# A graph layer's segment sums on TensorE: one full-width product per edge tile, or seven on four column quarters

## The chip, the cores and the metric

The kernel runs on one core of a Trainium2 chip, in fp32 throughout. The metric is device time in microseconds (us) of one execution; three runs of the kernel before took 5686.64, 5694.77 and 5710.15 us.

## The reference

12500 nodes carry 160 channels: 64 scalars and 32 vectors of three components. 400000 edges, sorted by their destination, each carry a source node, 16 numbers (`e16`) and 4 numbers (`e4`).

```python
h = relu(layernorm(x))                                   # [12500, 160]
x0, x1 = h[:, :64], h[:, 64:].reshape(n, 32, 3)
s0, y0 = x0 @ W_sc0 * a / 8, x0 @ W_l1_0 * a / 8         # a: one number per node
s1, y1 = the same of x1 with W_sc1, W_l1_1, / sqrt(32)
w = silu(e16 @ fc_W1 / 4) @ fc_W2 / 8                    # [400000, 192]
w_a, w_b, w_c, w_d = w[:, :64], w[:, 64:128], w[:, 128:160], w[:, 160:]
e0, e1 = e4[:, :1], e4[:, 1:]
mid_a = w_a * y0[src] * e0                               # 64
mid_d = w_d * (y1[src] . e1) / sqrt(3)                   # 32
mid_b = (w_b * y0[src])[:, :, None] * e1[:, None, :]     # 64 x 3
mid_c = (w_c * e0)[:, :, None] * y1[src]                 # 32 x 3
z0 = segment sum over dst of [mid_a, mid_d]              # 96 per node
z1 = segment sum over dst of [mid_b, mid_c]              # 96 x 3 per node
out0 = C_S * s0 + C_X * z0 @ W_l2_0 * a * const          # 96 -> 64
out1 = C_S * s1 + C_X * z1 @ W_l2_1 * a * const          # 96 -> 32, for each of three components
result = x + [out0, out1]
```

The indices `src` and `dst` are known only at run time.

## The kernel before

**Node stage.** The 98 tiles of 128 nodes are normalised, turned and mapped; `y0, y1` go to the scratch `y_d` in DRAM, the rest into the table `acc` in SBUF. Weights are loaded here, on SP's queue, by `edge_weight_loads` (L201), and scaled by DVE in `edge_weights` (L219). Among them is `wo`, three slabs of 128 rows by 160 columns, which holds W_l2_0 and three copies of W_l2_1 laid out for the 384 sums of a node.

**Edge stage.** The 3125 tiles of 128 edges are taken four at a time: 782 blocks. Three consecutive tiles (a window) touch at most 32 consecutive nodes in the ordinary case; four windows, 12 tiles, three blocks, are a group, and there are 261 groups. For a block b the functions are these:

- `load` (L403): SP fetches `e16`, and POOL issues four gathers (L417), one per tile, of 128 rows of 160 numbers from `y_d`, into `yg`. There are ten yg buffers, and the loads run eight blocks ahead; each POOL gather of a new buffer waits until DVE is done with the block that had it.
- `hidden_pair` (L434): PE's first edge product (L426) and ACT's silu (L431), for four blocks at a time.
- `weigh` (L440): PE makes the 192 edge weights of each tile (L448, two row halves of the array), and ACT scales 96 of them by e0 (L368) and writes e1 and the edge's place in its window beside them (L369). The result stays in PSUM; two such buffers.
- `select` (L472): DVE writes, for each tile, a matrix of 128 edges by 4 x 32 columns: the fourth part has a one where the edge goes to that node of the window, the first three parts are it times a component of e1 (L479, L481).
- `products` (L484): six DVE instructions (L374 to L381) make the 256 numbers `pr` of each edge: columns 0 to 63 mid_a, 64 to 95 mid_d, 96 to 191 mid_c by component, 192 to 255 w_b * y0.
- `sums` (L491): one PE product per tile, stationary the 128 columns of `sel`, moving the 256 of `pr`; three tiles add up in a PSUM bank (two such banks). Rows 96 to 127 of the result hold the sums with the plain ones, of which columns 0 to 191 are wanted; rows 0 to 95 hold those times e1's components, of which columns 192 to 255 are wanted. ACT takes these four pieces out in four instructions per window (L504, three of L506) and lays them as 32 rows of 384 in `zs`.
- After a group, in the three blocks that follow: `turn` (L509) transposes `zs` in three pieces (L514) and ACT copies the result (L516); `linear` (L519) makes three PE products with `wo` (L523), ACT copies the result (L525), and DVE makes `place` (L527); `add` (L530) distributes the rows over two node tiles by PE (L535), and `accumulate` (L538) reads a register that tells which node tiles, and adds them into `acc` with two DVE instructions (L544).

**Order.** PE, ACT and DVE run in the order in which the program is written (a manual schedule); the tile framework sets the semaphores. In the loop over blocks (L568) the order is: load(b + 8), weigh(b + 2), one of turn, linear, add for the group before, select and products of b + 1, accumulate in a group's third block, sums(b), and hidden_pair in every fourth block. An fp32 matmul stands in the profile as two passes, each a weight load (PEld) and a product (PE). A last part of the program (from L600) deals with tiles whose nodes lie too far apart; it keeps `wo` and isn't entered with these inputs.

Of the kernel before, what the change touches and what calls it, by code (L numbers as in the profile page):

```python
# [10 lines left out]
F32 = mybir.dt.float32  # L11
I32 = mybir.dt.int32
AF = mybir.ActivationFunctionType
ALU = mybir.AluOpType
# [4 lines left out]
P = 128  # L19
M0 = 64  # L20
M1 = 32
# [4 lines left out]
PC = 256  # L26
ZC = 384
GT = 4
BT = 32
WN = 32  # L30
WT = 3
GW = 4
TG = WT * GW
EG = 8
GN = 8
HN = 2
LO = D - P
EPS = 1e-5
C_S = math.sin(math.pi / 8.0)
# [4 lines left out]
def kernel(  # L44
# [19 lines left out]
    nc = tc.nc  # L64
# [3 lines left out]
    T = n_edges // P  # L68
# [13 lines left out]
    const = ctx.enter_context(tc.tile_pool(name="const", bufs=1))  # L82
# [5 lines left out]
    ident = const.tile([P, P], F32, name="ident")  # L88
# [90 lines left out]
    w1 = const.tile([P, 2 * FC_H], F32, name="w1")  # L179
    w2 = const.tile([P, NW], F32, name="w2")  # L180

    wo = const.tile([P, 3, D], F32, name="wo")
    wnr = ip.tile([P, 2, 3 * M1], F32, name="wnr")
    wor = ip.tile([P, 3, D], F32, name="wor")
# [16 lines left out]
    def edge_weight_loads():  # L201
        nc.gpsimd.memset(w1, 0.0)
        for i in range(P // FC_IN):
            nc.sync.dma_start(w1[FC_IN * i:FC_IN * (i + 1), FC_H * (i % 2):FC_H * (i % 2 + 1)], fc_w1)
        for i in range(2):
            for to, of, m in ((0, 0, M0), (M0, 2 * M0, M1), (M0 + M1, M0, M0), (2 * M0 + M1, 2 * M0 + M1, M1)):
                nc.sync.dma_start(w2[FC_H * i:FC_H * (i + 1), to:to + m], fc_w2[:, of:of + m])
        nc.gpsimd.memset(wor, 0.0)

        def o1(c):  # L210
            return slice(M0 + M1 * c, M0 + M1 * (c + 1))

        nc.sync.dma_start(wor[0:M0 + M1, 0, 0:M0], w_l2_0)
        for rows, k, c in ((slice(96, P), 0, 0), (slice(0, 32), 1, 1), (slice(32, 64), 1, 2)):
            nc.sync.dma_start(wor[rows, k, o1(c)], w_l2_1[M0:, :])
        for rows, k, c in ((slice(64, P), 1, 0), (slice(0, 64), 2, 1), (slice(64, P), 2, 2)):
            nc.sync.dma_start(wor[rows, k, o1(c)], w_l2_1[0:M0, :])

    def edge_weights():  # L219
        nc.vector.tensor_scalar(w2, w2, 1.0 / math.sqrt(FC_H), None, ALU.mult)  # L220
        f = C_X / math.sqrt(10.0 * (M0 + M1))
        nc.vector.tensor_scalar(wo[:, :, 0:M0], wor[:, :, 0:M0], f, None, ALU.mult)
        nc.vector.tensor_scalar(wo[M0:M0 + M1, 0, 0:M0], wo[M0:M0 + M1, 0, 0:M0], 1.0 / math.sqrt(3.0), None, ALU.mult)
        nc.vector.tensor_scalar(wo[:, :, M0:].rearrange("p k (u c) -> p k c u", c=3),
                                wor[:, :, M0:].rearrange("p k (c u) -> p k c u", c=3), f, None, ALU.mult)
# [27 lines left out]
    with (  # L253
# [82 lines left out]
        with tc.manual_schedule(engines=engines):  # L336
# [7 lines left out]
            last = len(steps) - 1  # L344
# [38 lines left out]
    with (  # L383
# [16 lines left out]
        def windows_of(g):  # L400
            return min(GW, NWIN - g * GW)
# [87 lines left out]
            prs[b] = pr  # L489

        def sums(b):  # L491
            pr = prs.pop(b)
            for k, t in enumerate(tiles_of(b)):
                g, w = t // TG, t // WT % GW
                if t % WT == 0:
                    z_ps[g, w] = p_z.tile([P, 512], F32, name="pz")
                pz = z_ps[g, w]
                last = t % WT == WT - 1 or t == T - 1
                nc.tensor.matmul(pz[:, 0:PC], sels[g][:, t % TG, :, :], pr[:, k, :], start=t % WT == 0, stop=last)  # L499
                if last:  # L500
                    if w == 0:
                        z_sb[g] = post.tile([P, ZC], F32, name="zs")
                    pz, zs = z_ps.pop((g, w)), z_sb[g][WN * w:WN * (w + 1), :]
                    nc.scalar.activation(zs[:, 0:192], pz[96:P, 0:192], AF.Copy)  # L504
                    for c in range(3):
                        nc.scalar.activation(zs[:, 192 + M0 * c:192 + M0 * (c + 1)],  # L506
                                             pz[WN * c:WN * (c + 1), 192:PC], AF.Copy)

        def turn(g):  # L509

            m, zs = WN * windows_of(g), z_sb.pop(g)
            pt = p_x.tile([P, 3, P], F32, name="px")
            for k in range(3):
                nc.tensor.transpose(pt[:, k, :m], zs[:m, P * k:P * (k + 1)], ident[:m, :m])  # L514
            za = post.tile([P, 3, P], F32, name="za")
            nc.scalar.activation(za[:, :, :m], pt[:, :, :m], AF.Copy)  # L516
            zT[g] = za

        def linear(g):  # L519
            m, za = WN * windows_of(g), zT.pop(g)  # L520
            po = p_x.tile([P, D], F32, name="px")
            for k in range(3):
                nc.tensor.matmul(po[:m, :], za[:, k, :m], wo[:, k, :], start=k == 0, stop=k == 2)  # L523
            os = post.tile([P, D], F32, name="os")
            nc.scalar.activation(os[:m, :], po[:m, :], AF.Copy)  # L525
            place = post.tile([P, 2, P], F32, name="place")
            nc.vector.tensor_scalar(place.rearrange("p h n -> p (h n)"), iota, at[:, g:g + 1], None, ALU.is_equal)  # L527
            o_sb[g] = os, place
# [205 lines left out]
```

## Time and profile before

| what | us |
|---|---|
| three runs, median | 5694.77 |
| the profiled execution, its own time | 5716.56 |
| its span in the profile | 5714.8 |
| PE busy, products / weight loads | 3840.1 / 2679.8 |
| DVE busy | 2902.1 |
| ACT busy | 2645.1 |
| POOL busy | 3024.8 |
| PE idle before the turn (L514), most of it until ACT's L504 | 876.2 |
| DVE idle before L479, most of it until ACT's L369 | 951.5 |
| mean TensorE clock granted, share of full | 0.776 |

Busy times are those of one engine in one execution. PE's products are pipelined, so their durations overlap and their sum isn't time at the peak; what a pass costs is seen better in the distance of starts, or in how long a row of them lasts. "Idle before" is time in which the engine had nothing under way ahead of that instruction, and the name behind the arrow is what the profile takes to have ended the wait; "remote" means that it finds no releaser close to the moment the wait ended. A queue's own rows carry a q (SPq). The clock is a mean over stretches: in some the array runs at full speed, in others at half.

### The profile page before, as it was taken

The page shows a single profiled execution, that of the slowest core. Times are in us where ns is not written, and L with a number is a line of the kernel's source. Part 1 is how long each engine was busy: PE and PEld are TensorE (multiplying, and loading weights), DVE is VectorE, ACT ScalarE, POOL GpSimd, SP SyncE. Part 2 cuts the span into 40 slices and gives each one's busy share as a digit, 9 for nine tenths or more (in the row PEclk, how much of TensorE's full clock was granted, in tenths as well). Part 3 has the DMA queues.
Part 4 walks back from the last instruction along what each step waited for, and adds up shares of the span by engine and source line. Part 5 has one row for each costly group of instructions (what it writes and reads, how often), then busy time and mean ns, then how long its engine had stood idle before and what let it go on. Part 6 is the DMA issues. An engine that isn't in the chain of part 4 may idle for free.

```text
span 5714.8 us, 61466 instructions
## 1 busy us (share of the span) xinstructions
PE 3840.1 (67%) x17265; PEld 2679.8 (47%) x17265; DVE 2902.1 (51%) x7407; ACT 2645.1 (46%) x9217; POOL 3024.8 (53%) x3150
## 2 busy tenths in 40 slices
PE   6476676666666666666667667666667766666766
PEld 5344444444444444444444445444444444444544
DVE  7454455444455455454555445544445554545555
ACT  5244444444444444444444444444444444444445
POOL 3655555555555555555555555555555555555553
PEclk9677777787777777777777777777777778788778
DMA  4211111211111111111112112111111121232211
GB/s 140 62 53 52 53 54 49 54 52 52 52 51 54 52 53 52 52 53 50 54 53 55 51 53 55 52 52 52 51 52 52 54 54 53 54 88 55 55 49 54
DMA packets 233168, 319.85 MB, mean 56 GB/s; under 512 B 65754, under 2 KB 182566, under 8 KB 232566
## 3 DMA queue, kind: packets, MB, share of 16 engines
q0 software_dynamic: 150000, 256.20, 16.7%
q1 hardware_dynamic: 69026, 51.24, 3.1%
q10 hardware_dynamic: 13796, 8.44, 0.5%
q8 instruction: 139, 2.28, 0.2%
q14 instruction: 207, 1.70, 0.1%
HBM read 299.62 MB, written 16.00 MB: 55 GB/s over the span
## 4 chain that ended last, share of the span: by engine, by line
PE 52%; another core or an unknown queue 23%; ACT 13%; issue 8%; DVE 3%; DMA 0%; SPq 0%; DVEq 0%; ACTq 0%
PE pz L499 25%; PE pw L448 10%; PE px L426 6%; ACT pw L368 5%; PE px L514 4%; PE px L523 4%; ACT zs L506 3%; PE px L535 3%; ACT zs L504 2%; ACT pw L369 1%; ACT hT L431 0%; DVE h L283 0%; DVE tmp L376 0%; DVE tmp L374 0%
## 5 line engine op out<-in xcount | busy, mean ns | idle before, releaser
L417 POOL DMA_INDIRECT yg<-y_d,src_sb x3125 | 2983.4, 955 | 2542.2 <-DVE pr L381 1641.0
L499 PE MATMUL pz<-pr,sel 128*128 128x256 f32 x6250 | 1930.1, 462 | 151.1 <-ACT zs L506 114.2
L368 ACT ACTIVATE pw<-pw,ev 128x96 f32<-128x96 f32 x3125 | 985.3, 315 | 1679.1 <-remote 1048.8
L499 PEld LDWEIGHTS pz<-pr,sel 128*128 128x128 f32 x6250 | 1443.4, 242 | 406.4 <-ACT zs L506 132.4
L544 DVE SCALAR_TENSOR_TENSOR acc<-px,a_sb,acc 128x160 f32 x522 | 200.2, 384 | 1765.5 <-remote 1292.0
L514 PE MATMUL px<-ident,zs 128*128 128x128 f32 (+1 forms) x783 | 268.9, 428 | 876.2 <-ACT zs L504 804.3
L448 PE MATMUL pw<-w,hT 64*128 64x192 f32 x6250 | 839.2, 394 | 12.9 <-DVE pr L381 8.1
L448 PEld LDWEIGHTS pw<-w,hT 64*128 64x128 f32 x6250 | 579.6, 216 | 469.4 <-issue 269.8
L426 PE MATMUL px<-xe,w 32*128 32x512 f32 x782 | 415.6, 789 | 526.1 <-remote 422.1
L479 DVE TENSOR_TENSOR sel<-iota,pw 128x128 f32<-128x128 f32 x782 | 223.5, 286 | 951.5 <-ACT pw L369 591.7
L504 ACT ACTIVATE zs<-pz 32x192 f32<-32x192 f32 x1042 | 337.8, 324 | 776.2 <-PE pz L499 312.9
L506 ACT ACTIVATE zs<-pz 32x64 f32<-32x64 f32 x3126 | 669.8, 214 | 41.8
L514 PEld LDWEIGHTS px<-ident,zs 128*128 128x128 f32 (+1 forms) x783 | 130.3, 181 | 1025.9 <-ACT zs L504 857.1
L376 DVE TENSOR_REDUCE tmp<-tmp 128x128 f32<-128x384 f32 x782 | 463.5, 593 | 26.8
L481 DVE TENSOR_TENSOR sel<-sel,pw 128x384 f32<-128x384 f32 x782 | 432.5, 553 | 26.7
L379 DVE TENSOR_TENSOR pr<-pw,yg 128x384 f32<-128x384 f32 x782 | 427.9, 547 | 0.0
L374 DVE TENSOR_TENSOR tmp<-yg,pw 128x384 f32<-128x384 f32 x782 | 427.8, 547 | 0.0
L426 PEld LDWEIGHTS px<-xe,w 32*128 32x128 f32 x782 | 107.8, 227 | 678.2 <-remote 470.9
L535 PE MATMUL px<-os,place 128*128 128x160 f32 x1044 | 236.7, 354 | 207.0 <-issue 175.0
L431 ACT ACTIVATE hT<-px 128x512 f32<-128x512 f32 x391 | 221.6, 596 | 300.5 <-remote 194.0
L377 DVE TENSOR_TENSOR pr<-pw,yg 128x256 f32<-128x256 f32 x782 | 323.6, 414 | 0.0
L378 DVE TENSOR_TENSOR pr<-pw,yg 128x256 f32<-128x256 f32 x782 | 323.4, 414 | 0.0
(83 smaller groups left out, 1902.3 us busy)
## 6 DMA issues: line engine op xcount, KB each, us to landing
yg<-y_d,src_sb POOLq DMA_INDIRECT x3125
xe<-in_e SPq DMA_DIRECT2D x784, 32.0 KB
xt<-in_x SPq DMA_DIRECT2D x12, 640.0 KB
y_d<-ys ACTq DMA_DIRECT2D x12, 640.0 KB
out<-acc SPq DMA_DIRECT2D x11, 640.0 KB
raw<-in_e SPq DMA_DIRECT2D x32, 192.0 KB
dst_i<-in_dst SPq DMA_DIRECT2D x1, 1568.0 KB
src_sb<-in_src SPq DMA_DIRECT2D x1, 1568.0 KB
```

The source lines that it names most:

```text
L368: nc.scalar.activation(pw[:, k, 0:96], pw[:, k, 0:96], AF.Copy, scale=ev[:, k, 0:1])
L374: nc.vector.tensor_tensor(tmp[:, :n, 0:3, :], y1, wt[:, :n, NW:NW + 3].unsqueeze(3).to_broadcast([P, n, 3, M1]), ALU.mult)
L376: nc.vector.tensor_reduce(tmp[:, :n, 3, :], tmp[:, :n, 0:3, :].rearrange("p t c u -> p t u c"), AX.X, ALU.add)
L379: nc.vector.tensor_mul(pr[:, :n, 96:192].rearrange("p t (c u) -> p t c u", c=3), wt[:, :n, M0:96].unsqueeze(2).to_broadcast([P, n, 3, M1]) ...
L417: nc.gpsimd.indirect_dma_start(out=yg[:, k, :], out_offset=None, in_=y_d, in_offset=bass.IndirectOffsetOnAxis(ap=src_sb[:, t:t + 1], axis=0))
L426: nc.tensor.matmul(ph, w1[r, :], xe[r, :], start=True, stop=True)
L448: nc.tensor.matmul(pw[:, k, 0:NW], hT[r, o:o + P], w2[r, :], start=True, stop=True)
L481: nc.vector.tensor_tensor(sel[:, :, 0:3, :], sel[:, :, 3:4, :].to_broadcast([P, n, 3, WN]), wt[:, :n, NW:NW + 3].unsqueeze(3).to_broadcast ...
L499: nc.tensor.matmul(pz[:, 0:PC], sels[g][:, t % TG, :, :], pr[:, k, :], start=t % WT == 0, stop=last)
L504: nc.scalar.activation(zs[:, 0:192], pz[96:P, 0:192], AF.Copy)
L506: nc.scalar.activation(zs[:, 192 + M0 * c:192 + M0 * (c + 1)], pz[WN * c:WN * (c + 1), 192:PC], AF.Copy)
L514: nc.tensor.transpose(pt[:, k, :m], zs[:m, P * k:P * (k + 1)], ident[:m, :m])
```

## The change

`sums` no longer makes one product of 128 by 256 per tile. The 128 columns of PE are taken as four quarters of 32. Each quarter collects 96 channels for the 32 nodes of a window: quarters 0 to 2 one vector component each (64 columns of w_b * y0 with `sel` times that component, and 32 columns of mid_c of that component with the plain `sel`), quarter 3 the 96 scalar ones. That is seven products per tile. The four windows of a group lie side by side in one bank, 4 x 96 columns, and ACT takes all out in one instruction after the group's last tile. `turn` transposes 96 columns of each window, four pieces; in the result a quarter's channels lie on 96 partitions for all 128 nodes of the group. `linear` multiplies each quarter with its own map, 96 by 64 or 96 by 32, from a new weight tile `wz` (two more DMAs on SP and two more DVE scalings), and ACT writes the result in two instructions, the second of which puts the components in their order. `wo` stays for the last part.

```diff
+    wz = const.tile([M0 + M1, M0 + M1], F32, name="wz")
...
+        nc.sync.dma_start(wz[:, 0:M0], w_l2_0)
+        nc.sync.dma_start(wz[:, M0:], w_l2_1)
...
+        nc.vector.tensor_scalar(wz, wz, f, None, ALU.mult)
+        nc.vector.tensor_scalar(wz[M0:, 0:M0], wz[M0:, 0:M0], 1.0 / math.sqrt(3.0), None, ALU.mult)
...
         def sums(b):
             pr = prs.pop(b)
             for k, t in enumerate(tiles_of(b)):
                 g, w = t // TG, t // WT % GW
-                if t % WT == 0:
-                    z_ps[g, w] = p_z.tile([P, 512], F32, name="pz")
-                pz = z_ps[g, w]
-                last = t % WT == WT - 1 or t == T - 1
-                nc.tensor.matmul(pz[:, 0:PC], sels[g][:, t % TG, :, :], pr[:, k, :], start=t % WT == 0, stop=last)
-                if last:
-                    if w == 0:
-                        z_sb[g] = post.tile([P, ZC], F32, name="zs")
-                    pz, zs = z_ps.pop((g, w)), z_sb[g][WN * w:WN * (w + 1), :]
-                    nc.scalar.activation(zs[:, 0:192], pz[96:P, 0:192], AF.Copy)
-                    for c in range(3):
-                        nc.scalar.activation(zs[:, 192 + M0 * c:192 + M0 * (c + 1)],
-                                             pz[WN * c:WN * (c + 1), 192:PC], AF.Copy)
+                if t % TG == 0:
+                    z_ps[g] = p_z.tile([P, 512], F32, name="pz")
+                sel = sels[g][:, t % TG, :, :]
+                first, last = t % WT == 0, t % WT == WT - 1 or t == T - 1
+                for r, part, c, lo, n in [(s, s, 192, 0, M0) for s in range(3)] + [(3, 3, 0, 0, SC)] + \
+                        [(s, 3, SC + M1 * s, M0, M1) for s in range(3)]:
+                    o = SC * w + lo
+                    nc.tensor.matmul(z_ps[g][WN * r:WN * (r + 1), o:o + n], sel[:, part, :], pr[:, k, c:c + n],
+                                     start=first and lo == 0, stop=last and (lo > 0 or r == 3))
+                if t % TG == TG - 1 or t == T - 1:
+                    zs = post.tile([P, GW, SC], F32, name="zs")
+                    n = windows_of(g)
+                    nc.scalar.activation(zs[:, :n, :].rearrange("p w c -> p (w c)"), z_ps.pop(g)[:, 0:SC * n], AF.Copy)
+                    z_sb[g] = zs

         def turn(g):
-            m, zs = WN * windows_of(g), z_sb.pop(g)
-            pt = p_x.tile([P, 3, P], F32, name="px")
-            for k in range(3):
-                nc.tensor.transpose(pt[:, k, :m], zs[:m, P * k:P * (k + 1)], ident[:m, :m])
-            za = post.tile([P, 3, P], F32, name="za")
-            nc.scalar.activation(za[:, :, :m], pt[:, :, :m], AF.Copy)
+            n, zs = windows_of(g), z_sb.pop(g)
+            pt = p_x.tile([P, GW, P], F32, name="px")
+            for w in range(n):
+                nc.tensor.transpose(pt[0:SC, w, :], zs[:, w, :], ident)
+            za = post.tile([SC, 4, GW, WN], F32, name="za")
+            nc.scalar.activation(za.rearrange("p s w n -> p w s n")[:, :n, :, :],
+                                 pt[0:SC, :n, :].rearrange("p w (s n) -> p w s n", n=WN), AF.Copy)
             zT[g] = za

         def linear(g):
-            m, za = WN * windows_of(g), zT.pop(g)
+            m, n, za = WN * windows_of(g), windows_of(g), zT.pop(g)
             po = p_x.tile([P, D], F32, name="px")
-            for k in range(3):
-                nc.tensor.matmul(po[:m, :], za[:, k, :m], wo[:, k, :], start=k == 0, stop=k == 2)
+            for r, lo, wd, o in [(3, 0, M0, 0)] + [(s, M0, M1, M0 + M1 * s) for s in range(3)]:
+                nc.tensor.matmul(po[:m, o:o + wd], za[:, r, :n, :], wz[:, lo:lo + wd], start=True, stop=True)
             os = post.tile([P, D], F32, name="os")
-            nc.scalar.activation(os[:m, :], po[:m, :], AF.Copy)
+            nc.scalar.activation(os[:m, 0:M0], po[:m, 0:M0], AF.Copy)
+            nc.scalar.activation(os[:m, M0:].rearrange("p (u c) -> p c u", c=3),
+                                 po[:m, M0:].rearrange("p (c u) -> p c u", c=3), AF.Copy)
```

Here `P` = 128, `WN` = 32 nodes of a window, `WT` = 3 tiles of a window, `GW` = 4 windows of a group, `TG` = 12, `M0` = 64, `M1` = 32, `SC` = 96.

More of the change, by code (lines that the diff above doesn't have):

```diff
@@ L36 @@
 HN = 2
+SC = M0 + M1
 LO = D - P
```

## The prediction

> **What bounds the kernel now.** I read the page's engine sums and groups first, then the waits, then the order of time in one group of three blocks near the middle, then the last stretch of the run. In the groups and waits, the columns after the bar are busy us, mean ns of one, then the idle time before them and what ended it; a line of waits gives total us, times, longest.
>
> ```profile
> PE 3840.1 (67%) x17265; PEld 2679.8 (47%) x17265; DVE 2902.1 (51%) x7407; ACT 2645.1 (46%) x9217; POOL 3024.8 (53%) x3150
> ...
> L417 POOL DMA_INDIRECT yg<-y_d,src_sb x3125 | 2983.4, 955 | 2542.2 <-DVE pr L381 1641.0
> L499 PE MATMUL pz<-pr,sel 128*128 128x256 f32 x6250 | 1930.1, 462 | 151.1 <-ACT zs L506 114.2
> ...
> L504 ACT ACTIVATE zs<-pz 32x192 f32<-32x192 f32 x1042 | 337.8, 324 | 776.2 <-PE pz L499 312.9
> L506 ACT ACTIVATE zs<-pz 32x64 f32<-32x64 f32 x3126 | 669.8, 214 | 41.8
> ```
>
> No engine is full. But POOL's row accounts for the span by itself: its 3125 gathers are busy 2983.4 us and idle 2542.2 us in between, 5525.6 together, of 5714.8. The gathers are listed from 136.8 us, and the last one starts at 5659.7 us, so 137 us lie before them and 54 us after. Of the idle time, 883.2 us is the 0.3 us between two gathers; the part that can move is the 1641.0 us in which POOL waits for a yg buffer, that is for L381, the last product.
>
> ```profile
> POOL yg L417 <- DVE pr L381: 1641.0, 282, 10.3
> DVE acc L544 <- remote: 1292.0, 166, 9.7
> ACT pw L368 <- remote: 1048.8, 161, 18.7
> POOL yg L417 <- issue: 883.2, 2805, 2.1
> ```
>
> There are 282 such waits for 261 groups, so about one per group, of 1641.0/282 = 5.82 us. A group needs 12 gathers at about 1.254 us, 15.05 us, and 15.05 + 5.82 = 20.9 us is the group's period. What DVE and ACT wait for meanwhile, the profile calls remote. The timeline (start, us, engine, line) shows it:
>
> ```profile
> 2505.70 0.81 PE L535 MATMUL px<-os,place 128*128 128x160 f32 x4
> ...
> 2508.17 0.92 PE L448 MATMUL pw<-w,hT 64*128 64x192 f32 x8
> ...
> 2510.89 1.36 ACT L368 ACTIVATE pw<-pw,ev 128x96 f32<-128x96 f32 x4 [5.79 <-remote]
> 2510.96 0.95 POOL L417 DMA_INDIRECT yg<-y_d,src_sb  x1 [0.30 <-issue]
> ...
> 2513.73 0.80 DVE L544 SCALAR_TENSOR_TENSOR acc<-px,a_sb,acc 128x160 f32 x2 [6.60 <-remote]
> ...
> 2516.14 3.00 PE L499 MATMUL pz<-pr,sel 128*128 128x256 f32 x8
> ...
> 2517.46 0.28 DVE L381 TENSOR_TENSOR pr<-pw,tmp 128x128 f32<-128x128 f32 x1
> ...
> 2517.81 1.01 POOL L417 DMA_INDIRECT yg<-y_d,src_sb  x1 [5.89 <-DVE pr L381]
> ```
>
> L544 needs L535, which had ended at 2506.51, and starts 7.2 us later, 1.8 us after POOL's last gather (ends 2511.91). So results of PE reach the others late while POOL issues a long run of gathers, and are let through when the run has drained. I don't know why; the profile shows that it happens. The circle is: POOL stops because its ten buffers are full; 1.8 us later DVE goes on; 4.0 us later L381 frees a buffer; POOL issues again. The last stretch has no gathers, and tells what the other engines can do alone:
>
> ```profile
> core 0: us, PE busy (x) PEld busy (x) DVE busy (x) ACT busy (x) POOL busy (x), PEclk, DMA share, GB/s
> ...
> 5672.00:5704.00 32.00, 31.30 (x173) 22.96 (x171) 27.45 (x77) 25.66 (x94) 0.00 (x0) 1.00 0.00 1
> ```
>
> There L544 comes at 5675.79, 5686.86 and 5697.81: 11.0 us a group at clock 1.00. So PE's work isn't the bound in the main stretch; the change can act only through POOL's 5.8 us gap.
>
> **The change, part by part.** *Sums on PE.* A 128x256 pass of L499 takes 216 ns at full clock (eight in 1.89 us less the last one's tail) and up to 427 at half clock (as in the 3.00 us above); a tile has two passes, 432 ns, a block of four 1.73 us. The new form has seven products of 64, 64, 64, 96, 32, 32, 32 columns, 14 passes and 14 weight loads a tile, 87,500 instructions in place of 12,500. By 216/256 = 0.84 ns a column each quarter streams 2 x 96 x 0.84 = 162 ns a tile. Lower bound: the four quarters run side by side, 162 ns a tile, 0.65 us a block. A nearby row says this can be: L448 has eight passes of 192 columns on two row halves, 8 x 162 = 1.30 us in series, yet they take 0.92 us. In series the columns make 2 x (3 x 54 + 81 + 3 x 27) = 648 ns a tile, 2.6 us a block. Upper bound: each pass waits for a load like a full one. L523, six passes in 1.08 us, has 160 columns and so 135 ns each; taking that for each of 14 passes gives 1.9 us a tile, 7.6 us a block. The load's length seems to follow its columns:
>
> ```profile
> L523 PEld LDWEIGHTS px<-wo,za 128*128 128x128 f32 x1560 | 232.9, 200 | 95.6 <-issue 54.9 <-ACT hT L431 26.9 <-ACT zs L506 10.6
> ...
> L523 PEld LDWEIGHTS px<-wo,za 128*64 128x64 f32 x6 | 0.7, 136 | 0.6 <-ACT za L516 0.6
> ```
>
> 64 columns less is 64 ns less, so a load of 32 should be short. I take 0.3 us a tile, 1.2 us a block, nearer the lower end, because L448 is the nearest in kind.
>
> The Trainium skill (TensorEngine Tiling, Instruction Overhead) speaks against the change: some 60 cycles of overhead for each matmul on trn2, and no tiling factor from a dimension already small. As an estimate from that page, 14 x 60 cycles at 2.4 GHz would be 350 ns a tile, 1.4 us a block if the overheads didn't overlap, hardly under the 1.73 of now; the 0.92 us of L448 can't decide it, since its passes are long.
>
> *Evacuation on ACT.* 4168 instructions (337.8 + 669.8 = 1007.6 us) become 261 of 128x384, 486 ns each by L516: 127 us. ACT loses 880 us, 1.1 us a block. It isn't on POOL's circle by itself; it stands in ACT's order ahead of the next scales (L368). PE's waits for a bank (L499 after ACT zs L506, 114.2 us) go: two banks now hold two whole groups. The new wait is the turn's, for the one evacuation after a group's last tile; before, the last window had four instructions (324 + 3 x 214 = 966 ns), now one of 486. Behind the turn on PE stand the next sums and the next weigh, for which ACT waits; this comes 0.5 us sooner.
>
> *Turn, linear, out.* Four transposes for three, +429 ns a group on PE by L514. The za copy 96x512 for 128x384, 596 (L431) for 486, +0.1 us on ACT. The linear has eight passes of 32 to 64 columns for six of 160, 0.8 to 1.1 us: no difference. The os copy becomes two, 292 to about 2 x 230, +0.17 us. In all +0.4 on PE and +0.3 on ACT a group; ACT's lost 3.4 us and the slack of PE cover both. Without that cover it would be 0.7 us x 261 = 183 us.
>
> *Setting up.* Two more DMAs on SP (24 and 12 KB), ahead of the other weights and of later loads of x, about 0.4 us of issue each (other SP issues show 0.35 to 0.43), and two DVE scalings at some 0.26 us (L222): 0 to 1.3 us once, taken as 0.
>
> **The sum.** The new circle is POOL's 15.05 us and the gap. The gap's parts: 1.8 us after the last gather, L544 0.80, then select and products, from 2514.45 to 2517.74, 3.3 us. The first and last are untouched: 5.1 us is the floor of a gap in which everything else is ready (L544 can lie in front of the run). Above it are 0.7 us x 282 = 203 us, in which DVE waits for L544 or for ACT's late scales (DVE sel behind ACT L369 591.7 us and L368 241.7 in all, many of them here). With sums some 0.5 us a block shorter, more at half clock, and ACT 1.1 us a block freer, the weights of the next blocks are scaled before the run holds PE's results back. Lower end of the gain: 0. Upper: 203, and more if runs grow (below). I take three quarters, 150 us, and in the tail 8 us, since DVE is busy 27.45 of 32 us there and 14% of 54 us is all there is. 5714.8 - 158 = 5557 us of span; the profiled execution took 5716.56, 22 us over the median of the runs, so **5537 us**, rounded 5540, against 5694.77. Without rival cases the range is 5480 to 5660.
>
> **Rivals.** *Quarters too slow (slower).* If the 14 passes go one after another or are held by loads, PE becomes late. In series a block costs 2.6 us at full clock and 5.1 at half. Decisive is when PE posts the weights of the third block of a run: now it does so some 7 us after the release, behind turn, sums, hidden and weigh; if it misses the stretch in which its results still pass, a run has two blocks. Then there are 391 gaps for 282, 109 x 5.82 = +635 us, 6330. Half the runs: +320, 6010. Beyond about (20.9 - 7.4)/3 = 4.5 us a block (7.4 us being PE's other work in a group: 3 x 0.92 + 1.6 + 1.1 + 0.8 + 1.1) PE is the bound itself; at 6.1 us a block 25.7 us a group, 6.7 ms. For it: short passes, many instructions, a mean clock of 0.776. Against: L448. I put it at **6100**.
>
> *Runs grow (faster).* PE and ACT being quicker, a fourth L381 comes before the results are held back, and the 1641 us of gaps shrink by a quarter: -410 - 8, **5280**. For it: DVE alone needs 3.3 us a block. Against: L544 waits once a group for L535 and holds DVE there; 261 groups and 282 gaps look locked to it.
>
> *Nothing.* PE and ACT are cheaper where they had slack and the circle keeps its 5.8 us: **5690**, or the quarters don't overlap and the slack takes that up.
>
> **How the numbers follow.** Forecast (gain of 1 to 4%) 0.37; quarters too slow 0.35; runs grow 0.14; nothing 0.12; 0.02 for something slower that I don't see. Under 0.5%, 28 us, no change can be told from the spread of the runs shown (5686.64 to 5710.15). Faster 0.37 + 0.14 = 0.51, same 0.12, slower 0.37. The range leaves out the worst of the slow case and the best of the fast one: 5230 to 6250.
>
> **What would show it.** Right: POOL's wait for L381 falls to some 1490 us at about 280 times; the sums' passes of one block take 0.6 to 1.8 us; ACT's zs group is near 130 us; L544's wait stays near 1300. Wrong: the number of POOL's waits changes (near 390: too slow; near 210: runs grow), or PE's sums take over 2.6 us a block, or the remote waits vanish, and with them the circle: then the bound is 15.05 us a group and the time could fall far below the range.

## The result and the profile after

The changed kernel took 6413.48 us (median of four runs, 6376.53 to 6433.92) against 5690.87 for the kernel before (four runs): a ratio of **1.123, 95% interval 1.1184 to 1.1276**. It is slower by 12%, and 6413 lies outside the forecast range. The profiled execution has a span of 6432.1 us, 717.3 more than before.

The page of the changed kernel, engines and groups (busy us, mean ns of one, idle time before them and what ended it):

```profile
PE 4263.1 (66%) x55546; PEld 2910.2 (45%) x55546; DVE 2887.5 (45%) x7409; ACT 1796.0 (28%) x5571; POOL 3023.2 (47%) x3150
...
L424 POOL DMA_INDIRECT yg<-y_d,src_sb x3125 | 2981.9, 954 | 3260.9 <-DVE pr L388 2409.4
L512 PE MATMUL pz<-pr,sel 128*32 128x64 f32 (+2 forms) x43750 | 1707.2, 260 | 1604.9 <-issue 1591.4
...
L517 ACT ACTIVATE zs<-pz 128x384 f32<-128x384 f32 (+1 forms) x261 | 127.2, 487 | 763.0 <-remote 381.0
```

And its waits (us in total, times, longest):

```profile
POOL yg L424 <- DVE pr L388: 2409.4, 392, 11.9
PEld pz L512 <- issue: 2138.9, 3029, 4.1
...
PE pz L512 <- issue: 1591.4, 2406, 3.2
ACT pw L375 <- PE pw L455: 1422.5, 534, 15.5
...
POOL yg L424 <- issue: 839.3, 2700, 1.6
```

POOL's row shows where the time went. The gathers are as busy as before (2981.9 for 2983.4 us). POOL's wait for a buffer, behind the last product (L381 before, L388 now), went from 1641.0 us in 282 waits to 2409.4 in 392: +768.4. The small idle time between two gathers fell by 43.9. Together that is +724.5 us, and the span grew by 717.3.

The second thing to see is a wait that the kernel before hardly had: "issue" ahead of PE's sums (L512), 1591.4 us in 2406 pauses, where L499 before had 36.2 us in 28. Two waits of the kernel before:

```profile
PE px L535 <- issue: 175.0, 67, 5.4
...
PE pz L499 <- issue: 36.2, 28, 3.0
```

In these waits PE waits for nothing that the profile shows. The order of time in one block of the changed kernel (start, us, engine, line):

```profile
2817.21 0.95 POOL L424 DMA_INDIRECT yg<-y_d,src_sb  x1 [0.30 <-issue]
...
2817.48 1.19 PE L512 MATMUL pz<-pr,sel 128*32 128x64 f32 x42
...
2818.88 0.40 PE L512 MATMUL pz<-pr,sel 128*32 128x64 f32 x3 [0.21 <-issue]
...
2819.60 0.27 PE L512 MATMUL pz<-pr,sel 128*32 128x64 f32 x1 [0.32 <-issue]
...
2820.30 0.54 PE L512 MATMUL pz<-pr,sel 128*32 128x64 f32 x10 [0.44 <-issue]
```

A block has 4 x 14 = 56 passes. 42 run off in 1.19 us; then three, one and ten come at 2818.88, 2819.60 and 2820.30, 0.7 us apart, while their operands have long been there. PE isn't slow here: it starts its next passes late. That it isn't given its instructions is a reading, since the profile names no releaser; the experiments test it. The step of 0.7 us is the rule: of 2405 distances between such pauses, 1096 are 0.7 to 0.8 us and 664 are 1.4 to 1.5. From the first pass's start to the last one's, a block's sums take 4.00 us in the mean (median 2.28; one block in ten over 12.3), and before they took 2.23 (median 1.51).

In some series of runs (the runs of one experiment and of the kernel before beside it) the kernel before takes 5690 to 5840 us ("held" below) and in the others 4070 to 4074 ("free"; medians), steady within a series, and chip 9 showed 5808 in one series and 4074 in a later one, so that it isn't a property of the chip alone. The forecast and its result are from a held series.

### The profile page after: what moved, and what is told of

Same layout as the page of the kernel before. It is cut to its first block, busy times and chain, and to the rows that moved or that the text cites. A ratio compares the mean times of both kernels' runs of the same rounds, so it can differ in the third digit from the quotient of the medians.

```text
span 6432.1 us, 134643 instructions
## 1 busy us (share of the span) xinstructions
PE 4263.1 (66%) x55546; PEld 2910.2 (45%) x55546; DVE 2887.5 (45%) x7409; ACT 1796.0 (28%) x5571; POOL 3023.2 (47%) x3150
## 4 chain that ended last, share of the span: by engine, by line
PE 58%; issue 27%; another core or an unknown queue 8%; ACT 3%; DVE 3%; DMA 0%; SPq 0%; POOL 0%; ACTq 0%; DVEq 0%
PE pz L512 23%; PE pw L455 16%; PE px L433 6%; PE px L535 5%; PE px L549 4%; PE px L525 3%; ACT pw L375 1%; ACT hT L438 1%; DVE h L290 0%; DVE tmp L381 0%; ACT zs L517 0%; DVE tmp L383 0%; DVE acc L558 0%; DVE pr L386 0%
## 5 line engine op out<-in xcount | busy, mean ns | idle before, releaser
L424 POOL DMA_INDIRECT yg<-y_d,src_sb x3125 | 2981.9, 954 | 3260.9 <-DVE pr L388 2409.4
L512 PE MATMUL pz<-pr,sel 128*32 128x64 f32 (+2 forms) x43750 | 1707.2, 260 | 1604.9 <-issue 1591.4
L512 PEld LDWEIGHTS pz<-pr,sel 128*32 128x32 f32 x43750 | 1187.4, 139 | 2158.4 <-issue 2138.9
L375 ACT ACTIVATE pw<-pw,ev 128x96 f32<-128x96 f32 x3125 | 985.3, 315 | 2717.2 <-PE pw L455 1422.5
L455 PE MATMUL pw<-w,hT 64*128 64x192 f32 x6250 | 1214.9, 485 | 157.3 <-issue 125.2
L455 PEld LDWEIGHTS pw<-w,hT 64*128 64x128 f32 x6250 | 806.0, 270 | 539.1 <-issue 418.2
L381 DVE TENSOR_TENSOR tmp<-yg,pw 128x384 f32<-128x384 f32 x782 | 427.8, 547 | 0.0
L549 PE MATMUL px<-os,place 128*128 128x160 f32 x1044 | 355.6, 489 | 39.8 <-ACT hT L438 27.3
L535 PE MATMUL px<-wz,za 96*128 96x32 f32 (+1 forms) x2088 | 331.4, 304 | 29.6 <-ACT hT L438 13.9
L535 PEld LDWEIGHTS px<-wz,za 96*128 96x128 f32 x2088 | 299.9, 219 | 100.8 <-issue 63.0
L517 ACT ACTIVATE zs<-pz 128x384 f32<-128x384 f32 (+1 forms) x261 | 127.2, 487 | 763.0 <-remote 381.0
L549 PEld LDWEIGHTS px<-os,place 128*128 128x128 f32 x1044 | 255.5, 305 | 152.6 <-issue 97.5
L525 PE MATMUL px<-ident,zs 128*96 128x128 f32 x1042 | 241.0, 375 | 71.0 <-ACT zs L517 70.8
```

The lines of the kernel that those rows point to most:

```text
L375: nc.scalar.activation(pw[:, k, 0:96], pw[:, k, 0:96], AF.Copy, scale=ev[:, k, 0:1])
L381: nc.vector.tensor_tensor(tmp[:, :n, 0:3, :], y1, wt[:, :n, NW:NW + 3].unsqueeze(3).to_broadcast([P, n, 3, M1]), ALU.mult)
L424: nc.gpsimd.indirect_dma_start(out=yg[:, k, :], out_offset=None, in_=y_d, in_offset=bass.IndirectOffsetOnAxis(ap=src_sb[:, t:t + 1], axis=0))
L455: nc.tensor.matmul(pw[:, k, 0:NW], hT[r, o:o + P], w2[r, :], start=True, stop=True)
L512: nc.tensor.matmul(z_ps[g][WN * r:WN * (r + 1), o:o + n], sel[:, part, :], pr[:, k, c:c + n], start=first and lo == 0, stop=last and (lo > ...
L525: nc.tensor.transpose(pt[0:SC, w, :], zs[:, w, :], ident)
```

## The experiments

### Without gathers, or with plain loads

**e1, e2**: only the first ten blocks are gathered; all later ones use their rows again. The same edit in both kernels:

```
+        kept = {}
...
+            if b >= 10:
+                rows[b] = kept[b % 10]
+                return
             yg = ygp.tile([P, GT, D], F32, name="yg")
-            rows[b] = yg
+            rows[b] = kept[b] = yg
```

> The changed kernel with gathers for the first ten blocks only; every later block multiplies the rows that those ten buffers hold, so the output isn't the layer's. Theory (PE gets its instructions and its results out slowly while POOL issues gathers): the pauses inside the sums vanish, the passes of a tile take the 0.32 us that they show where they run without a pause, and a group takes what DVE needs, some 11 us, so 261 x 11 + 250 = about 3100 us, and no slower than the kernel before without its gathers. Rival (the quarters themselves are slow, in the array or through the low clock): the sums keep some 3 us a block and the kernel stays about 12% slower than the one before without gathers.

> The kernel before with gathers for the first ten blocks only; the output isn't the layer's. Both theories: the last stretch of the profile before, where no gathers were left, had 11.0 us a group, so about 261 x 11.0 + 250 = 3120 us, and no waits for results of PE that had long been done. If such waits stay, the gathers aren't what holds PE's results back.

Measured: 3101.61 us changed (three runs that agree; a fourth took 3141.83) and 3071.45 before; the unedited kernel before took 4072.66 in this (free) series, and the ratios to it are 0.7612 and 0.7541. So the gathers set the time in a free series. Without them the changed kernel is about 1% slower, where it was expected to be no slower. What the change costs in a held series can't be read from this pair, nor whether POOL's issuing or the transfers matter.

**e10, e11** tell these apart. POOL's 3125 gathers become 3125 plain loads on SP's queue, of the same size:

```
-                nc.gpsimd.indirect_dma_start(out=yg[:, k, :], ...)
+                i = t % (NT - 1)
+                nc.sync.dma_start(yg[:, k, :], y_d[i * P:(i + 1) * P, :])
```

> The changed kernel with the 3125 gathers of POOL replaced by 3125 plain loads of 128 rows in a row on SP's queue, so that it computes with other rows; same bytes, same landings. Theory 'POOL's issue of gathers is what binds (4073 us) and, where the kernel before takes 5690 us, what holds PE back': 3050 to 3500 in both places, DVE near 90%, no pauses of PE in the sums. Rival 'the rows' transfers and their landings do it': about 4000 or more where the kernel before takes 4073, over 5500 where it takes 5690.

> The same edit in the kernel before; other rows than the reference's too. Theory: 3050 to 3500, and within 2% of the changed kernel with the same edit, since DVE (2900 us busy) is then the bound in both and the change leaves DVE alone. Rival 'the transfers': about 4000 or more, or over 5500, as in the other run. If this one is over 2% slower than the changed kernel with plain loads, the change gains as soon as POOL doesn't bind.

This series was held: the unedited kernel before took 5808.27 us. With plain loads the changed kernel took 3113.69 (0.5364 of it, 0.5351 to 0.5377) and the kernel before 3071.63 (0.529, 0.5278 to 0.5302). The transfers are the same 256 MB, and of the loss of 12% there is 1.4% left. It is **the gathers that POOL issues** that hold, not the amount of data. The edit changes more than the issuing engine: the gathers' own descriptors and their scattered rows are gone too, and these runs don't tell the three apart. From the timelines of the two, the sums of one block, the changed kernel first:

```profile
1500.65 0.90 PE L511 MATMUL pz<-pr,sel 128*32 128x64 f32 x56
```

```profile
1500.19 1.89 PE L498 MATMUL pz<-pr,sel 128*128 128x256 f32 x8
```

Without pauses the 56 passes take half of what the eight took. Still the changed kernel is 1.4% slower here. DVE is busy 91% of the span in it and 93% in the kernel before, PE 84% and 96%; and PE, with less to do, ran at a granted clock of 0.906 for 0.988. What makes the 1.4%, the clock or DVE's waits, isn't shown.

### The number of instructions

**e5**: the changed kernel unedited. **e3, e6, e12**: four products of 96 columns a tile in place of seven, 16 PE instructions (passes and loads) for 28, before 4. **e4, e7**: nine products, 36 instructions, by `[(3, 3, M1 * i, M1 * i, M1) for i in range(3)]` in the place of `[(3, 3, 0, 0, SC)]`. The edit for four:

```
-    for r, part, c, lo, n in [(s, s, 192, 0, M0) for s in range(3)] + [(3, 3, 0, 0, SC)] + \
-            [(s, 3, SC + M1 * s, M0, M1) for s in range(3)]:
+    for r, part, c, lo, n in [(s, s, 160, 0, SC) for s in range(3)] + [(3, 3, 0, 0, SC)]:
...
-                     start=first and lo == 0, stop=last and (lo > 0 or r == 3))
+                     start=first, stop=last)
```

> Four products of 96 columns on the quarters instead of seven of 64, 96 and 32: 8 passes a tile for 14, the same 96 columns for each quarter, the same evacuation, turn and maps; the first 32 columns of three quarters hold a wrong product. Theory (the number of PE's instructions is what costs): half of the way back from 14 passes to 2, by 720/12 = 60 us for a pass per tile, about 6050 us. Rival (array time of the quarters, clock): the columns are the same, so 6300 to 6420 us. Rival (turn, maps or the one evacuation cost it): 6413 us, unchanged.

> The fourth quarter's product of 96 columns split in three of 32: nine products, 18 passes a tile, the same columns. Theory (number of PE's instructions): 4 x 60 us more, about 6650 us. Rivals (array time; turn, maps, evacuation): 6413 us, within 1%.

> The changed kernel as it is. Where the kernel before takes about 5690 us (gathers hold back PE's results) all theories expect 6380 to 6440, with some 390 waits of POOL for L388. Where it takes about 4073 us (gathers in one unbroken run), POOL's 3125 gathers at 1.254 us are the bound and the change should take 4060 to 4090, ratio 1.00: the changed kernel itself hasn't been run there yet. If it is over 4150 there, the change costs something that POOL's run doesn't hide.

> Four products of 96 columns a tile in place of seven: 16 PE instructions a tile (passes and loads) for 28, before 4; the first 32 of the 96 columns of three quarters hold other sums than wanted. Theory 'number of PE instructions under gathers': half of the added 24 is gone, so where the kernel before takes about 5690 us this takes 5950 to 6200, with 320 to 360 waits of POOL. Rival 'quarters or the new ends as such': 6300 to 6430. Where the kernel before takes about 4073 us: 4060 to 4090 by both.

> Nine products a tile, the fourth quarter's 96 columns in three products of 32: 36 PE instructions a tile for 28, the same columns in all. Theory 'number of PE instructions under gathers': where the kernel before takes about 5690 us, 8 more instructions for the 24 that cost 720 us: 6550 to 6750. Rival 'quarters or the new ends as such': 6380 to 6450. Where the kernel before takes about 4073 us: 4060 to 4090 by both.

Both of these series (e3 and e4; e5, e6 and e7) were free, so what was expected for a held one wasn't tested, and nothing made a difference: ratios to the kernel before of 1.000 (0.9991 to 1.001) and 1.0005 for four and nine in the first, 1.0003 (0.9994 to 1.0013), 1.0005 and 1.0004 for seven, four and nine in the second. So **the same two kernels that differ by 12% in a held series are equal in a free one.** Groups of e5 (the changed kernel, free):

```profile
L424 POOL DMA_INDIRECT yg<-y_d,src_sb x3125 | 2962.7, 948 | 952.7 <-issue 768.3
...
L381 DVE TENSOR_TENSOR tmp<-yg,pw 128x384 f32<-128x384 f32 x782 | 432.4, 553 | 980.6 <-DMA yg<-y_d,src_sb 957.3
L512 PE MATMUL pz<-pr,sel 128*32 128x64 f32 (+2 forms) x43750 | 930.5, 250 | 0.3 <-DVE pr L388 0.3
```

POOL's wait for a buffer is gone. It issues one gather after another, 2962.7 + 952.7 = 3915 us, and DVE waits for rows instead of POOL for buffers. PE's passes of the sums wait 0.3 us in all.

**e9**, the kernel before unedited, for its profile:

> The kernel before as it is, for its profile. Where it takes about 4073 us: POOL's gathers in one run with no wait for L381, the sums of a block in at most 2.2 us at the granted clock, fewer than 50 late posts of PE, and DVE waiting for gathers as in the profiles of the changed kernel there. If instead PE's posts come late here too and POOL's waits for L381 are many, then the time of 4073 us has another cause than posts that come on time. Where it takes about 5690 us: the page of before again, 270 to 300 waits for L381.

It took 4072.11 us (free).

```profile
L417 POOL DMA_INDIRECT yg<-y_d,src_sb x3125 | 2961.5, 948 | 953.4 <-issue 773.9
...
L374 DVE TENSOR_TENSOR tmp<-yg,pw 128x384 f32<-128x384 f32 x782 | 432.5, 553 | 1022.9 <-DMA yg<-y_d,src_sb 1021.3
```

The same ledger as e5's: that is why they are equal. Of PE's posts (the moments at which a result is announced to other engines) 2 of 3392 came over 0.12 us after the end of the matmul that makes them; in the profile of before it was 1504 of 3080, by 1.63 us in the mean over all. (The counts are of posts on record that can be put to a matmul; how that is done moves them by 1 to 2%.) The changed kernel is slower although its posts are less late: in the profile of after some 550 of 2230, by 0.79 us in the mean. The sums took 1.66 us a block from first to last start, 0.97 in e5.

**e8** cuts the product of the kernel before into four of 64 columns on the whole array:

```
-  nc.tensor.matmul(pz[:, 0:PC], sels[g][:, t % TG, :, :], pr[:, k, :], ...)
+  for o in range(0, PC, PC // 4):
+      nc.tensor.matmul(pz[:, o:o + PC // 4], sels[g][:, t % TG, :, :], pr[:, k, o:o + PC // 4], ...)
```

> The kernel before with its product of 256 columns cut into four of 64, on the whole array as before, ACT's evacuation, turn and linear as before: 16 PE instructions a tile for 4, the same columns in all. Theory 'number of PE instructions under gathers': where the kernel before takes about 5690 us, this is slower too, 5950 to 6250, without any column quarter. Rival 'quarters or the new ends': 5680 to 5760. Where the kernel before takes about 4073 us: 4060 to 4090 by both, unless loads of 128 columns (8 x 0.2 us a tile, 6.4 us a block) make PE the bound, then 1.6 x 3125 = 5000 or more.

It landed in a free series, so its question stayed open, but it took 4431.71 us, ratio 1.0882 (1.0863 to 1.09), with PE busy 98%, below the 5000 named for loads as the bound.

```profile
2501.66 3.68 PE L500 MATMUL pz<-pr,sel 128*128 128x64 f32 x32
```

32 passes on the whole array take 3.68 us, 3.41 from first to last start, 110 ns each; e5's 56 on quarters went at 0.70 us when the clock was full (the fastest tenth of its blocks), 13 ns each. So the short passes were cheap on different quarters, and not on the whole array.

**e12** repeats the four products, and hit a held series:

> Four products of 96 columns a tile for seven (the first 32 columns of three quarters hold other sums): 16 PE instructions a tile for 28, before 4. Theory 'number of PE instructions under gathers': where the kernel before takes 5690 to 5810 us, ratio 1.04 to 1.08. Rival 'quarters or the new ends as such': 1.11 to 1.14. Where it takes about 4073: 1.00 by both.

6069.03 us against 5838.76: **1.0386 (1.0364 to 1.0409)**, for 1.123 with seven. With half of the added instructions gone, two thirds of the loss are gone, so the ratio lies just under the theory's 1.04 to 1.08. The rival's 1.11 to 1.14 is out, for the quarters, the turn, the maps and the single evacuation are all still there. The granted clock isn't the main cause either: it is 0.661 here and was 0.646 with seven products. The 1.123 is from another held series; seven products weren't run in this one. POOL's waits for the last product are 2042.5 us in 380, and the issue waits ahead of the sums fell from 1591.4 to 839.3:

```profile
POOL yg L424 <- DVE pr L388: 2042.5, 380, 9.6
...
PE pz L511 <- issue: 839.3, 1249, 3.2
```

So the loss falls with the number of PE's instructions. How the 3.9% that are left divide between the remaining instructions, the clock and the new ends isn't shown.

### Letting POOL pause

If PE's results and instructions are held back while POOL issues gathers, then idle work on POOL should make the kernel faster.

**e13**: five memsets (128x480) after the gathers of every second block of the kernel before.

```
+        idle = post.tile([P, 480], F32, name="idle")
...
+            if b % 2 == 1:
+                for _ in range(5):
+                    nc.gpsimd.memset(idle, 0.0)
```

> The kernel before with five memsets of POOL (128x480, some 0.49 us each) after the gathers of every second block, so that POOL issues no gather for about 2.4 us after each eight. Where the kernel before takes about 4073: POOL is the bound, 391 x 2.4 = 940 us more, 4950 to 5050. Where it takes 5690 to 5810, theory 'results of PE are held back while POOL issues gathers and pass when it pauses': faster in spite of the added work, 4900 to 5500. Rival 'POOL's waits for buffers are set by the other engines' own time': no faster, 5690 to 5900, the memsets lie in the waits.

5918.62 us against 5838.76, ratio 1.013: by its time a miss for the theory. But the profile shows another edit than was meant: nothing tied the memsets to their blocks, and all 1955 ran in the first 3141 us, some 2.2 us after each four gathers. That makes two kernels of one. POOL's waits in the first part, 600 to 3000 us, with memsets, and then in 3300 to 5700, without:

```profile
POOL yg L419 <- issue: 350.8, 1171, 2.1
POOL yg L419 <- DVE tmp L374: 21.6, 101, 0.5
POOL yg L419 <- DVE tmp L376: 6.3, 30, 0.2
```

```profile
POOL yg L419 <- DVE pr L381: 748.6, 123, 10.0
POOL yg L419 <- issue: 374.5, 1187, 1.5
```

With pauses the wait for the last product isn't there at all, and 69 of 964 posts of PE were late; without, 654 of 1318. So pauses do let results pass; these, of 2.2 us, were only as long as the waits that they removed (7.38 us for four gathers and 7.20).

**e14, e15, e16, e17, e18** tie shorter pauses to each block, by clearing a part of the buffer that its gathers then fill: two, three or one memsets in the kernel before (e14, e15, e17), three and two in the changed one (e16, e18).

```
             rows[b] = yg
+            for _ in range(2):
+                nc.gpsimd.memset(yg[:, 0:3, :], 0.0)
             for k, t in enumerate(tiles_of(b)):
```

> The kernel before with two memsets of POOL (128x480, 0.49 us each) into a block's yg ahead of its four gathers: POOL issues no gather for 1.0 us after each four. POOL's own floor is then 137 + 782 x (5.02 + 1.1) = 4920 us. Theory 'PE's results pass when POOL pauses, and 1 us is enough': 4900 to 5200 where the kernel before takes 5690 to 5840. The same theory with a pause that is too short: 5500 to 5900. Rival 'POOL's waits are set by the other engines': 5690 to 5900. Where the kernel before takes about 4073: 4850 to 5000, a plain loss.

> The same with three memsets, 1.5 us after each four gathers; POOL's floor is 137 + 782 x (5.02 + 1.6) = 5310 us. Theory: 5250 to 5450 where the kernel before takes 5690 to 5840, with few late posts of PE (under 15%). Rival: 5690 to 5900. Where the kernel before takes about 4073: 5200 to 5400.

> The changed kernel with three memsets ahead of each block's gathers. Theory 'the change's loss is PE's instructions held back under gathers': where the kernel before takes 5690 to 5840, the pauses take the loss away: 5250 to 5600, at most 5% over the kernel before with the same pauses, and under 0.97 of the kernel before. Rival 'quarters or new ends cost PE or ACT time by themselves': 6300 to 6450 still. Where the kernel before takes about 4073: 5200 to 5400, as the kernel before with the same pauses.

One held series, the kernel before at 5808.16 us:

| run | us | ratio | posts over 0.12 us late | mean lateness |
|---|---|---|---|---|
| e14, before, 1.0 us | 4917.47 | 0.849 (0.8445 to 0.8535) | 2311 of 3200 | 0.83 us |
| e15, before, 1.5 us | 5247.13 | 0.9056 (0.9009 to 0.9104) | 111 of 2450 | 0.04 us |
| e16, changed, 1.5 us | 5444.25 | 0.9396 (0.9315 to 0.9476) | 416 of 2067 | 0.31 us |

Added idle work makes the kernel before 15% faster, as the theory expected, and its rivals (5690 to 5900, and 6300 to 6450 for e16) are out; e15 lies just under its 5250 to 5450. With 1 us more posts are late than without a pause, but by half as much in the mean (0.83 us for 1.63); with 1.5 us few are late. The waits of e14 and e15, POOL's in the one and DVE's in the other (in both L417 is the memset and L419 the gather):

```profile
POOL yg L419 <- issue: 729.5, 2724, 1.7
...
POOL yg L417 <- DVE pr L379: 99.6, 65, 3.4
```

```profile
DVE tmp L374 <- DMA yg<-y_d,src_sb: 2180.0, 754, 5.7
```

1641 us of waiting for a buffer (in the profile of before) have become 100. In e15 POOL is the bound, as in a free series: DVE waits for rows. The changed kernel with the same pauses is 3.8% slower (5444.25 for 5247.13), and its waits show where:

```profile
ACT pw L375 <- PE pw L457: 1609.6, 598, 10.4
PEld pz L514 <- issue: 1306.0, 2424, 1.3
```

ACT waits for weights from PE, and PE's loads for the sums still wait for nothing that the profile shows. The 56 passes took 2.90 us a block in the mean, for 4.00 without pauses; e15's eight took 1.93, for 2.23.

> The kernel before with one memset (0.5 us) ahead of a block's four gathers; POOL's floor is 137 + 782 x (5.02 + 0.6) = 4530 us. If half a microsecond is enough to let PE's results pass: 4500 to 4800 where the kernel before takes 5690 to 5840. If the held results need about the 1.8 us that a run of gathers takes to drain less some of it, it is too short: 5200 to 5900. Where the kernel before takes about 4073: 4450 to 4600, a plain loss.

> The changed kernel with two memsets (1.0 us) ahead of a block's gathers, POOL's floor 4920 us as in e14. Theory 'the change's loss is PE's instructions, which come in only while POOL pauses': less pause, fewer instructions, so slower than the same kernel with 1.5 us (5444) and 10% or more over e14's 4917: 5450 to 6100 where the kernel before takes 5690 to 5840. Rival 'a pause of 1 us lets all of it pass': 4900 to 5200. Where the kernel before takes about 4073: 4850 to 5000.

These two fell in a free series (the kernel before 4073.68) and so answer only for it: 4376.23 us, ratio 1.0743 (1.0722 to 1.0764), and 4774.13, 1.172 (1.1697 to 1.1743). Both are below what was expected: a block costs 0.39 and 0.90 us more, not 0.6 and 1.1. In a free series a pause is a plain loss, so no version with pauses beats both kernels in both kinds of series; in a held one e14 beats both, by 15% and by some 23% (4917 for 6413, from two series). How short a pause may be in a held series wasn't measured.

## Why the prediction was wrong

**What was right.** The place: the change acts only through POOL's wait for a buffer, which carries the whole difference. The evacuation: 1007.6 us became 127.2, -880.4 as worked out. The small terms: the za copy 576 ns for 486 (+0.09, forecast +0.1), os 212 + 294 for 293 (+0.21, forecast +0.17), the first gather 1.4 us later (138.2 for 136.8, forecast 0 to 1.3), which proves little, since in e9 the kernel before has it at 138.3.

**The step that failed** is the term of the sums: "I take 0.3 us/tile, 1.2 us a block, nearer the lower end, because L448 is the nearest in kind". As a price of *streaming* it holds: the 56 passes take 0.70 us at full clock and 1.26 at half. The trace of after has blocks like that too. But L448 has eight passes a block, the sums have 56, and while POOL issues gathers in a held series the cost goes with the number of PE's instructions (28 a tile: 12% slower, 16: 4%). The forecast counted them, 28 a tile for 4, and gave them no price under the gathers; the sums took 4.00 us a block in place of 1.2. The sign for it in the trace of before was faint: L535, four plain passes, waited 175.0 us in 67 pauses of up to 5.4 us for "issue", a row that e9 doesn't have; the forecast read "issue" on POOL's row and not on PE's.

**The next step fell with it.** "ACT 1.1 us a block freer, the weights of the next blocks are scaled before the run holds PE's results back": ACT waits for PE's weights, not for its own time (the scales wait 1422.5 us behind L455 by name and 907.9 remote, where all of ACT is busy 1796.0). What ACT saved was slack: it brought POOL's waits no gain.

**The rival "quarters too slow"** came true in its count and its place, and not in its cause. It said 391 gaps for 282 and +635 us; there are 392, and they grew from 5.82 to 6.15 us: 110 x 5.82 + 392 x 0.33 = 769. That each is a run of gathers cut short fits the runs' lengths: of 284 unbroken runs of gathers before, 234 had twelve; of 388 after, 116 had twelve, 149 eight, 121 four. But the passes neither go in series nor wait for loads. Its price was set at 6100, under its own full sum of 6330, and the range ended at 6250. The runs were in fact mixed, not all of two blocks, and each gap was longer, which the forecast's 5.82 us didn't allow for.

**The Trainium skill's rule** (TensorEngine Tiling, Instruction Overhead: some 60 cycles for each matmul on trn2) pointed to the right side for another reason. Its estimate was 1.4 us a block if overheads didn't overlap; 0.70 us shows that on quarters they do, 13 ns a pass. On the whole array e8 shows 110 ns a pass.

**"I don't know why."** The forecast took the late results as a fact of the kernel and put 1.8 and 3.3 us of each gap down as untouched. They are neither fixed nor the kernel's: plain loads take them away (3072 us), a pause of 1.5 us leaves 111 of 2450 late, and in e9, in a free series, there are 2 of 3392. Asking what holds them might have priced the edit: what holds PE's posts may hold its next instructions too.

**What stays open**: what makes a series held, and what PE's posts and instructions share with POOL's gathers. A slow fetch of instructions isn't seen. One instruction queue grew with PE's instructions, some 65 bytes for each, before and after:

```profile
q8 instruction: 139, 2.28, 0.2%
```

```profile
q8 instruction: 439, 7.19, 0.5%
```

Its transfers of 16 KB took 1.01 us in the median in the profile of after and 1.05 in e5, where nothing is held, and 92% of the pauses ahead of L512 have none of them under way. So if instructions are short, it is behind this transfer. Posts of all engines are also missing from held records: 3270 of 3670 are there for PE, 4432 of 5827 for DVE and 4736 of 6371 for ACT in the profile of before, and 3660, 5747 and 6343 in e9. Whether the recording itself takes part in the holding isn't known, for every run here has a record. The gathers themselves look alike in both kinds: 949 and 946 ns on POOL in the median, the last packet 2.21 and 2.27 us after the start. The new ends alone (turn, maps) weren't run in a held series without the quarters; e12, which has them, is 3.9% slower in all.

## What to carry to other kernels

Count instructions as well as their time: an edit that cuts one long matmul into many short ones can halve PE's time and still lose, where each instruction can be held up, as here under POOL's gathers. Pauses marked "issue" inside a run of like matmuls whose operands are ready (here L535 before, and then the sums 0.7 us apart) are the sign to look for before making them more. And when an engine seems idle for no reason, take away or slow down a *neighbour* in one run: 1 us of useless work on POOL bought 15% here in a held series, where 880 us saved on ACT bought none.

## What the hardware showed unexpectedly

- In held series half of PE's posts come late while POOL issues gathers one after another (1504 of 3080), while ACT's and DVE's are within 0.01 us for 99 of 100; in a free series it is 2 of 3392 (e9), and for the changed kernel some 160 of 2220, by 0.05 us in the mean (e5). The same kernel takes 5690 to 5840 or 4070 us.
- PE's passes then start in portions about 0.7 us apart, while the transfers of its instructions take 1.01 us, no longer than the 1.05 in a free series.
- Passes of 32 to 96 columns on four column quarters start 13 ns apart in the mean at full clock (56 in 0.70 us); passes of 64 columns on the whole array 110 ns (32 in 3.41 us).
- The granted clock fell with PE's work on the quarters: 0.937 before and 0.754 changed in free series (e9, e5), at the same time of 4070 us. The passes of the weights, which the change leaves alone (L448, L455), took 363 and 439 ns in the mean. So a part of what the quarters save on PE is given back.
